# Layer 3's transfers of changed-over keys and queries issued by SP instead of GpSimd

## The chip, the core and the metric

The kernel is one program on one core of a Trainium2 chip. The core has five engines that run their own instruction streams in order and wait for each other through semaphores: TensorE (PE, with its weight loads shown apart as PEld), VectorE (DVE), ScalarE (ACT), GpSimd (POOL) and SyncE (SP), which here does nothing but issue transfers. Transfers (DMAs) are issued by SP or by GpSimd and carried out by 16 DMA engines. The metric is the time of the program on the device in microseconds (us); lower is better. All data are float32.

## What is computed

The input `x` has 4 batches of 1024 rows of 256 numbers. Four layers follow each other, each as `x = x + f(layernorm(x))`: attention (layer 1), a feed-forward net (layer 2), a second attention (layer 3), the same feed-forward net (layer 4). The change is in layer 3, whose core is:

```python
h = layernorm(x) * ln_scale + ln_bias              # 256 wide
c_q, c_kv = h @ w_down_q.T, h @ w_down_kv.T        # 128 wide
q, k, v = c_q @ w_up_q.T, c_kv @ w_up_k.T, c_kv @ w_up_v.T   # 16 heads of 64
e, o = q[..., 0::2], q[..., 1::2]                  # q, and k in the same way
q = interleave(e * cos - o * sin, e * sin + o * cos)
attn = softmax(q @ k.T / 8)
out = (attn @ v) @ w_out.T + residual
```

The rotation in the fifth line needs, beside each element of a query or key, its neighbour in the pair (even with odd). It is this exchange that is called changed over here.

## The kernel before

**Tiling.** Both attention layers are made by the same function, `attention` (L181). It takes two heads at a time (a pair of heads; 8 of them in each of the 4 batches, so 32 pairs in a layer), with keys and queries held transposed: 128 partitions (two heads of 64) by 1024 positions. A pair has 8 steps, each of 128 query rows, so a layer has 256 steps. Two steps make a half, called `h` in the code, and the unit in which transfers go.

**A step.** `scores` (L229) multiplies queries with keys into PSUM; `exponentials` (L244) finds the negated maximum on DVE (L249) and the exponential on ACT (L251); `invert` (L257) makes the reciprocal sums; `turn` (L265) transposes the probabilities in 32x32 blocks on DVE (L271) into the tile `T`. The blocks are then in the wrong partitions, so the 16 squares of a half are moved by DMA, each 32 partitions of 4352 bytes, 136 KB, from `T` to `pT` (`send`, L289, issued at L295). In layer 3 one square is copied by ACT instead (`keep`, L285), 10 are issued by SP and 5 by GpSimd (`POOL_DMA = 5`). In layer 1 it is 11 and 5. `weigh` (L297) multiplies `pT` with the values, two halves later; `take` (L310) scales the sums on GpSimd (L316); `project` (L318) multiplies with the output weights (L167) and adds to `x` on GpSimd (L328).

**Order.** Nothing is scheduled by the compiler: each engine runs its instructions in the order in which the Python code emits them, and waits are put in where data or buffers demand it. The loop in `steps_with` (L330) emits a step; other work (projections of the next pair, loads of weights) is put between by a table `pieces` from step number to functions. A piece at a whole number is emitted last in its step; a piece at a number that is `EARLY` = 0.5 smaller is emitted earlier in the step, ahead of `weigh`, `take`, `turn` and the sending. In the odd steps these lines matter:

```python
            for f in pieces.get(s - EARLY, ()):
                f()
            ...
            if part == 0 and 0 <= s < n:
                send(s // HB, nc.sync, sent[: len(sent) - POOL_DMA])
            for f in pieces.get(s, ()):
                f()
```

GpSimd's five squares of that half are emitted in the next, even step, after its `scores` and ahead of `project`.

**Buffers.** `T` and `pT` have two buffers each. So the first transposition of a half must wait until all 15 squares of the half before last have been read out of their `T`, and the first square of a half must wait until `weigh` and `take` are through with the `pT` of the half before last. The tile `turned` has one buffer.

**Keys and queries of layer 3.** `pair_b` (L630) prepares the next pair during the steps of the present one. `load` (L633) brings three weight tiles by SP; `load_out` (L208) brings the output weights, also three transfers, also by SP. For keys (i = 1) and then queries (i = 0), each in two blocks of 512 positions, it does `qk` (L638: a product and a copy by ACT, L647), `change` (L649: two DMAs of 64 partitions of 2048 bytes, 128 KB each, that exchange even and odd partitions into `turned`) and `rotate` (L654: three operations on GpSimd, L657 to L659, with tables of cosine and sine). `qk` is at k - EARLY, `change` at k + 1, `rotate` at k + 2, with k = -2, 0, 2 and 4: one block in every two steps. The steps of `change` are odd. Both weight loads are also pieces of odd steps, at EARLY, each in one of the four odd steps of a pair.

Of the kernel before, what the change touches and what calls it, by code (L numbers as in the profile page):

```python
# [35 lines left out]
EARLY = 0.5  # L36
# [3 lines left out]
def hybrid_block_kernel(  # L40
# [5 lines left out]
    nc = tc.nc  # L46
# [12 lines left out]
    def group(*shape):  # L59
        last[0] ^= 1  # L60
        return ps_mm.tile([P, *shape], F32, tag=f"m{last[0]}", name="mm")
# [84 lines left out]
    def standardize(dst, src, shift, rstd):  # L146
        nc.scalar.activation(dst, src, AF.Identity, scale=rstd, bias=shift)  # L147

    def transposed(dst, src, c, affine=None):

        tr = group(TQ, P)
        for t in range(TQ):
            nc.tensor.transpose(tr[:, t, :], src[:, t, ts(c, P)], ident)  # L153
        trf = tr.rearrange("p t q -> p (t q)")
        if affine is None:
            nc.scalar.copy(dst[:, c, :], trf)  # L156
        else:
            nc.scalar.activation(
                dst[:, c, :], trf, AF.Identity,
                scale=affine[0][:, c : c + 1], bias=affine[1][:, c : c + 1],  # L160
            )

    def paired(out, parts, first=True, last=True):

        for i, (lhsT, rhs) in enumerate(parts):
            for j in range(2):
                nc.tensor.matmul(  # L167
                    out[ts(j, DH)], lhsT[:, ts(j, DH)], rhs[j],
                    start=(first and i == 0), stop=(last and i == len(parts) - 1),
                )  # L170

    def by_head(out, parts):

        for i, (lhsT, rhs) in enumerate(parts):
            for j in range(2):
                nc.tensor.matmul(  # L176
                    out[ts(j, DH)], lhsT, rhs[:, ts(j, DH)],
                    start=(i == 0), stop=(i == len(parts) - 1),
                )
# [404 lines left out]
    def layer_b(rows):  # L584

        scale_b = 1.0 / 8.0
        cs = {}

        def batch_b(b):
            work = []  # L590
            for qb in range(NQB):
                k = {}

                def first(t, b=b, k=k, qb=qb):
                    if t == 0:
                        if b:
                            k["x1"] = xnp.tile([P, TQ, D], F32, tag="xn", name="x1")
                        else:
                            k["x1"] = ptp.tile([P, SENT], F32, tag="pT", name="x1")[
                                :, : TQ * D  # L600
                            ].rearrange("p (t d) -> p t d", t=TQ)
                    xt = xs[b][:, qb * TQ + t, :]
                    standardize(k["x1"][:, t, :], xt, *rows.factors(NQB * b + qb, t)[:2])
                    nc.gpsimd.tensor_add(xt, xt, k["x1"][:, t, :])

                def second(t, b=b, k=k, qb=qb):
                    x1 = k["x1"][:, t, :]
                    nc.scalar.mul(x1, x1, rows.factors(NQB * b + qb, t)[2])

                def turned(c, b=b, k=k, qb=qb):  # L610
                    if c == 0:
                        p, tag = (highp, f"high{qb}") if b % 2 == 0 else (lowp, "low")
                        cs[b, qb] = p.tile([P, NC, QB], F32, tag=tag, name="hc")
                    transposed(cs[b, qb], k["x1"], c, affine=(lns_sb, lnb_sb))

                def down(m, b=b, qb=qb):

                    h = cs[b, qb][:, :, ts(m, QB // 2)]
                    pc = group(2, QB // 2)
                    for i in range(2):  # L620
                        paired(pc[:, i], [(wd_sb[:, i, c, :], [h[:, c]] * 2) for c in range(NC)])
                    nc.scalar.copy(h, pc)

                work += [(10 * qb - 8 + t, lambda t=t, f=first: f(t)) for t in range(TQ)]
                work += [(10 * qb - 6 + t, lambda t=t, f=second: f(t)) for t in range(TQ)]
                work += [(10 * qb - 2 + 2 * c - EARLY, lambda c=c, f=turned: f(c)) for c in range(NC)]
                work += [(((2, 8), (16, 18))[qb][m], lambda m=m, f=down: f(m)) for m in range(2)]
            return work

        def pair_b(b, pr):  # L630
            made, turned = {}, {}

            def load():  # L633
                w = made["w"] = wp.tile([P, 3, NC, P], F32, tag="w", name="w")[:, :, 0, :]
                for i, up in enumerate((wuq, wuk, wuv)):
                    nc.sync.dma_start(w[:, i], up[:, ts(pr, P)])  # L636

            def qk(i, qb):  # L638

                pq = group(QB)  # L640
                paired(pq, [(made["w"][:, i, :], [cs[b, qb][:, i]] * 2)])
                name = ("qT", "kT")[i]
                if qb == 0:
                    made[name] = qkp.tile([P, S], F32, tag=name, name=name)
                straight = made[name][:, ts(qb, QB)]
                made[i, qb] = straight
                nc.scalar.mul(straight, pq, (scale_b, 1.0)[i])  # L647

            def change(i, qb):  # L649
                turned[i, qb] = rp.tile([P, QB], F32, tag="turned", name="turned")  # L650
                for r in range(2):
                    nc.gpsimd.dma_start(turned[i, qb][r::2], made[i, qb][1 - r :: 2])

            def rotate(i, qb):  # L654

                straight, other = made[i, qb], turned.pop((i, qb))
                nc.gpsimd.tensor_mul(straight, straight, cos_sb[:, ts(qb, QB)])  # L657
                nc.gpsimd.tensor_mul(other, other, sin_sb[:, ts(qb, QB)])
                nc.gpsimd.tensor_add(straight, straight, other)  # L659

            def values(qb):
                if qb == 0:
                    made["v"] = vp.tile([P, NK2, DH], F32, tag="v", name="v")
                pv = group(NK2 // NQB, DH)
                for t in range(NK2 // NQB):
                    lhsT = cs[b, qb][:, 1, ts(t, DH)]
                    by_head(pv[:, t, :], [(lhsT, made["w"][:, 2, :])])
                nc.scalar.copy(made["v"][:, ts(qb, NK2 // NQB), :], pv)

            work = []  # L670
            for i in (1, 0):
                for qb in range(NQB):
                    k = 2 - 4 * i + 2 * qb
                    work += [(k - EARLY, lambda i=i, qb=qb: qk(i, qb))]
                    work += [(k + 1, lambda i=i, qb=qb: change(i, qb))]
                    work += [(k + 2, lambda i=i, qb=qb: rotate(i, qb))]
            work += [(4 + 2 * qb - EARLY, lambda qb=qb: values(qb)) for qb in range(NQB)]
            return {name: lambda name=name: made[name] for name in ("qT", "kT", "v")}, load, work

        return attention(batch_b, pair_b, wo_b, nc.sync, lead=5, kept=1)  # L680


# [73 lines left out]
```

## Time and profile before

| What | us |
|---|---|
| median of 3 runs | 3290.56 (3285.77 to 3292.66) |
| profiled execution, whole | 3286.08 |
| profiled execution, span | 3284.2 |
| steady part of layer 3 in the span | 1700 to 3040 |

In 1700 to 3040 the busy times are: TensorE 1296.20, VectorE 1217.16, GpSimd 1170.68, ScalarE 1017.49 us of 1340, with a DMA share of 0.88. TensorE's granted clock is 0.99 there.

The whole span has this by engine, and this by transfers (columns of the second: name of the tile written and read, engine that issues, number, size of one, median time from the start of the issue to landing):

```profile
PE 3204.3 (98%) x52736; PEld 2022.2 (62%) x52736; DVE 2531.7 (77%) x2386; ACT 2107.9 (64%) x4304; POOL 1958.5 (60%) x2738
```

```profile
pT<-T SPq DMA_DIRECT2D x2688, 136.0 KB, 4.7
pT<-T POOLq DMA_DIRECT2D x1280, 136.0 KB, 4.8
turned<-kT POOLq DMA_DIRECT2D x128, 128.0 KB, 3.5
turned<-qT POOLq DMA_DIRECT2D x128, 128.0 KB, 3.3
...
wo<-in_wo_b SPq DMA_DIRECT2D x32, 128.0 KB, 3.7
```

The busy share of TensorE is no measure of how close it is to its limit, since the ends of pipelined matmuls are modelled. Issues by SP are not counted as busy anywhere: the page shows SP only in the chain of waits (as SPq) and in the list of transfers, and the timeline shows when it issued what.

### The profile page before, as it was taken

To read this page: it belongs to the slowest core of one execution; us is meant where nothing else is said; L and a number is where in the kernel's file an instruction comes from. 1 tells how busy PE (TensorE), PEld (TensorE's weight loads), DVE (VectorE), ACT (ScalarE), POOL (GpSimd) and SP (SyncE) were. 2 spreads that over 40 slices of the span, in tenths; PEclk is the share of its full clock that TensorE was granted. 3 is DMA by queue.
4 is the path that set the end of the run, shared out by engine and by line. 5 is a ranking of instruction groups with operands and counts; after the bars stand their busy time and mean duration, and the time that the engine had idled before them with its cause. 6 is when DMAs were issued, how large, how long until landed. Compare 5 with 4: busy or idle time off the path is not lost.

```text
span 3284.2 us, 126564 instructions
## 1 busy us (share of the span) xinstructions
PE 3204.3 (98%) x52736; PEld 2022.2 (62%) x52736; DVE 2531.7 (77%) x2386; ACT 2107.9 (64%) x4304; POOL 1958.5 (60%) x2738
## 2 busy tenths in 40 slices
PE   8999999999999999999999999999999999998999
PEld 4666666666666666666555556666666666655666
DVE  7988888888888888941049889998999899998100
ACT  5666666666666666643447877787777777777332
POOL 4545454445544544430158889998889898986110
PEclk9999999999999999999999999999999999999999
DMA  8888888888888888840039889988888899987100
GB/s 227 226 218 219 223 225 221 221 220 229 222 216 217 224 221 227 216 112 1 4 87 238 222 222 243 244 240 231 237 237 239 232 246 244 241 240 212 39 20 20
DMA packets 244698, 642.13 MB, mean 196 GB/s; under 512 B 74305, under 2 KB 102977, under 8 KB 244129
## 3 DMA queue, kind: packets, MB, share of 16 engines
q1 hardware_dynamic: 161104, 397.60, 47.4%
q0 software_dynamic: 83024, 236.44, 25.6%
q8 instruction: 419, 6.86, 1.0%
q14 instruction: 151, 1.23, 0.1%
HBM read 43.39 MB, written 4.19 MB: 14 GB/s over the span
## 4 chain that ended last, share of the span: by engine, by line
PE 71%; SPq 12%; DMA 6%; DVE 4%; ACT 4%; issue 3%; POOL 1%; DVEq 0%; ACTq 0%; POOLq 0%
PE sc L238 20%; PE mm L304 19%; PE mm L167 15%; SPq L295 11%; PE mm L421 7%; PE ph L410 7%; DMA pT<-T 5%; PE mm L176 4%; DVE T L271 2%; DVE nmax L249 1%; ACT p L251 1%; POOL oT L316 1%; PE mm L153 1%; ACT gT L414 0%; SPq L636 0%
## 5 line engine op out<-in xcount | busy, mean ns | idle before, releaser
L249 DVE TENSOR_REDUCE nmax<-sc 128x1 f32<-128x1024 f32 x1024 | 1204.3, 1218 | 222.8 <-PE sc L238 219.7
L251 ACT ACTIVATE p<-sc,nmax 128x1024 f32<-128x1024 f32 x1024 | 1144.1, 1117 | 323.0 <-DVE nmax L249 323.0
L271 DVE STREAM_TRANSPOSE T<-p 128x2176 f32<-128x2176 f32 x512 | 1247.4, 2436 | 50.9 <-DMA pT<-T 24.6
L238 PE MATMUL sc<-kT,qT 64*64 64x512 f32 x8192 | 1087.2, 598 | 15.6 <-ACT p L251 10.5
L304 PEld LDWEIGHTS mm<-pT,v 64*64 64x64 f32 x32768 | 951.3, 133 | 141.7 <-issue 100.6
L304 PE MATMUL mm<-pT,v 64*64 64x128 f32 x32768 | 986.7, 269 | 10.3 <-issue 9.5
L295 POOL DMA_DIRECT2D pT<-T x1280 | 629.6, 499 | 120.8 <-PE sc L238 55.4
L316 POOL TENSOR_TENSOR oT<-oT,pT 128x256 f32<-128x256 f32 x256 | 186.2, 727 | 719.7 <-ACT oT L314 647.7
L238 PEld LDWEIGHTS sc<-kT,qT 64*64 64x64 f32 x8192 | 333.8, 133 | 413.8 <-issue 276.1
L328 POOL TENSOR_TENSOR x<-x,got 128x512 f32<-128x512 f32 x256 | 330.9, 1293 | 26.9 <-ACT got L326 22.9
L326 ACT COPY got<-mm 128x512 f32<-128x512 f32 x256 | 149.8, 585 | 282.0 <-PE mm L167 282.0
L428 DVE TENSOR_TENSOR x<-x,mm 128x512 f32<-128x512 f32 x32 | 22.0, 687 | 367.1 <-PE mm L421 367.1
L167 PE MATMUL mm<-wo,oT 128*64 128x256 f32 x2048 | 278.4, 393 | 19.9 <-POOL oT L316 18.7
L167 PEld LDWEIGHTS mm<-wo,oT 128*64 128x64 f32 x2048 | 124.6, 136 | 267.3 <-POOL oT L316 221.5
L260 ACT COPY p<-total 128x128 f32<-128x128 f32 x512 | 151.8, 297 | 203.7 <-DVE total L259 197.1
L414 ACT ACTIVATE gT<-ph,b_sb 128x512 f32<-128x512 f32 x128 | 87.4, 685 | 299.6 <-PE ph L410 299.5
L167 PE MATMUL mm<-hT,w 128*64 128x512 f32 x1024 | 243.3, 596 | 1.1 <-ACT hT L156 1.0
L421 PE MATMUL mm<-w_sb,gT 128*128 128x256 f32 x1024 | 226.0, 381 | 6.5 <-ACT hT L156 6.5
L410 PE MATMUL ph<-hT,w_sb 128*128 128x512 f32 x512 | 229.3, 601 | 0.2 <-ACT hT L156 0.2
L421 PEld LDWEIGHTS mm<-w_sb,gT 128*128 128x128 f32 x1024 | 193.1, 190 | 39.4 <-ACT hT L156 9.4
L396 POOL TENSOR_TENSOR x<-x,b_sb 128x256 f32<-128x256 f32 x64 | 44.5, 726 | 275.5 <-ACT xn L147 275.5
L251 ACT ACTIVATION_READ_ACCUMULATOR p<-sc,nmax 128x1 f32 x1024 | 205.0, 200 | 0.0
(90 smaller groups left out, 2471.4 us busy)
## 6 DMA issues: line engine op xcount, KB each, us to landing
pT<-T SPq DMA_DIRECT2D x2688, 136.0 KB, 4.7
pT<-T POOLq DMA_DIRECT2D x1280, 136.0 KB, 4.8
turned<-kT POOLq DMA_DIRECT2D x128, 128.0 KB, 3.5
turned<-qT POOLq DMA_DIRECT2D x128, 128.0 KB, 3.3
w<-in_wqkv_a POOLq DMA_DIRECT2D x96, 128.0 KB, 5.9
wo<-in_wo_a POOLq DMA_DIRECT2D x32, 128.0 KB, 5.1
wo<-in_wo_a POOLq DMA_DIRECT2D x64, 64.0 KB, 5.3
wo<-in_wo_b SPq DMA_DIRECT2D x32, 128.0 KB, 3.7
```

The source lines that it names most:

```text
L167: nc.tensor.matmul(out[ts(j, DH)], lhsT[:, ts(j, DH)], rhs[j], start=(first and i == 0), stop=(last and i == len(parts) - 1),)
L238: nc.tensor.matmul(sc[s, j][ts(half, DH), ts(m, 512)], qT()[rows, ts(2 * qs + half, DH)], kT()[rows, ts(m, 512)], start=True, stop=True,)
L249: nc.vector.tensor_reduce(nmax, sc[s, j], AX.X, ALU.max, negate=True)
L251: nc.scalar.activation(probs[s][:, :NK2, ts(j, 2), :], sc.pop((s, j)).rearrange("p (k c i) -> p k c i", c=2, i=SQ), AF.Exp, bias=nmax, acc ...
L260: nc.scalar.copy(probs[s][:, NK2].rearrange("p (j c) i -> p j (c i)", j=2), t.unsqueeze(2).to_broadcast([P, 2, DH]),)
L271: nc.vector.transpose(T[h][:, :, q, :, :].rearrange("p c k i -> p k c i"), probs.pop(s))
L295: engine.dma_start(pT[h][ts(c, SQ), a], T[h][ts(a, SQ), c])
L304: nc.tensor.matmul(av[h][q][ts(j ^ q, DH)], v[ts(j, DH), k, :], pT[h][ts(j, DH), :, q, k, :], start=(k == 0), stop=(k == NK2 - 1),)
L316: nc.gpsimd.tensor_mul(parts, parts, pT.pop(h)[:, :, :, NK2, :])
L328: nc.gpsimd.tensor_add(xd, xd, got)
L410: nc.tensor.matmul(ph, w1_sb[:, c, ts(f, P)], hT[n][:, c, :], start=(c == 0), stop=(c == NC - 1),)
L421: nc.tensor.matmul(po[n][:, t % 2, :], gT[n][:, f, ts(t, P)], w2_sb[:, f, :], start=(f == 0), stop=(f == NF - 1),)
```

## The change

`change` issues its two DMAs from SP (`nc.sync`) instead of GpSimd, and its place in the table goes from k + 1 to k + 1 - EARLY. It so stands in SP's stream ahead of the 10 squares of the same odd step and behind the 10 squares of the half before. Where an odd step also has a load, the three loads of output weights come ahead of `change`, and the three loads of the projection's weights behind it. Shapes, bytes, buffers and arithmetic stay as they are.

```diff
             def change(i, qb):
                 turned[i, qb] = rp.tile([P, QB], F32, tag="turned", name="turned")
                 for r in range(2):
-                    nc.gpsimd.dma_start(turned[i, qb][r::2], made[i, qb][1 - r :: 2])
+                    nc.sync.dma_start(turned[i, qb][r::2], made[i, qb][1 - r :: 2])
...
                     work += [(k - EARLY, lambda i=i, qb=qb: qk(i, qb))]
-                    work += [(k + 1, lambda i=i, qb=qb: change(i, qb))]
+                    work += [(k + 1 - EARLY, lambda i=i, qb=qb: change(i, qb))]
                     work += [(k + 2, lambda i=i, qb=qb: rotate(i, qb))]
```

## The prediction

> **What bounds the kernel now.** The change touches layer 3 alone, so I read the page for the whole span first and then each view for 1700 to 3040 us, the steady part of layer 3. The 254 transpositions (L271) in it start between 1700.7 and 3034.6: 5.27 us a step, 42.2 us a pair of heads, some 31.8 pairs. VectorE needs per step two maxima of 1.22, a transposition of 2.44 and a reciprocal of 0.12, 5.0 us: 95% of the step. So VectorE is nearly the bound, and what the kernel loses is 0.27 us a step in which it waits for others. Who these are, the chain of waits in that window tells first (shares by engine and line; SPq is SP issuing):
>
> ```profile
> by line: SPq L295 27.0%; PE sc L238 14.7%; PE mm L304 12.8%; DMA pT<-T 11.1%; PE mm L167 9.0%; issue 6.2%; DVE T L271 3.6%; DVE nmax L249 2.7%; ACT p L251 2.4%; PE mm L176 1.4%; POOL oT L316 1.2%; SPq L636 0.8%; SPq L214 0.7%; DMA w<-in_wuq
> ```
>
> SP's issuing of squares leads, with their flight behind it; GpSimd has 1.2%. The groups of L295 in the window (ns: least, median, most) show that a square costs SP anything from 0.5 to 2.3 us, and GpSimd always the same:
>
> ```profile
> L295 SPq DMA_DIRECT2D pT<-T x1270: 507/597/2333, 1699.1 to 3039.9; - x182
> L295 POOL DMA_DIRECT2D pT<-T x635: 489/492/553, 1709.0 to 3039.6; - x159
> ```
>
> The waits of SP in the window (total us, times, longest) show how little of SP is free, and the timeline of SP alone what it does in two pairs (start, us, what):
>
> ```profile
> SPq L295 <- DVE total L259: 57.0, 46, 3.5
> SPq L295 <- POOL oT L316: 14.8, 17, 3.5
> SPq L295 <- DVE T L271: 6.7, 3, 3.1
> SPq L295 <- DMA pT<-T: 4.6, 9, 0.9
> SPq L214 <- DMA pT<-T: 4.1, 6, 0.9
> ```
>
> ```profile
> 2347.70 20.04 SPq L295 DMA_DIRECT2D pT<-T  x20
> 2367.78 0.59 SPq L212 DMA_DIRECT2D wo<-in_wo_b  x1
> 2368.42 1.18 SPq L214 DMA_DIRECT2D wo<-in_wo_b  x2
> 2369.90 17.63 SPq L295 DMA_DIRECT2D pT<-T  x20
> ```
>
> With 1.5 us of smaller rows all its waits are 88.7 us of 1340: 2.8 us a pair. SP is issuing for the other 93%. Most of the free time lies in the two odd steps of a pair that have no load; where one has (half of them), the row after it shows the squares starting at once, late. And late squares cost: the next transposition but one half needs its tile read out. The waits of VectorE and TensorE in the window:
>
> ```profile
> DVE T L271 <- DMA pT<-T: 15.2, 21, 2.0
> ...
> DVE T L271 <- DMA wo<-in_wo_b: 3.3, 4, 1.3
> ```
>
> ```profile
> PE mm L167 <- POOL oT L316: 17.9, 25, 3.3
> ```
>
> With three smaller rows for landings of weights (which use the same semaphores) the transpositions lose 21.0 us. Where they lose nothing the margin is small: from the last landing of a half to the start of the transposition that needs its tile the median over 122 halves of the trace is some 0.7 us.
>
> **The change part by part.**
>
> *GpSimd loses 8 issues a pair.* The median is 0.570 us, so 256 are 146 us, in layer 3 1.14 us of every two steps (10.55 us), of which GpSimd is busy 87% (1170.68 of 1340). It isn't on the path except where it is late for L316: the 17.9 us above, in 25 places. Being 1.14 us earlier should take about half of that away, the other places being the batch edges, where it is up to 3.3 us late: **-9 us**. Its five squares start earlier by the same 1.14 us; they have 4 us to spare before their tile is needed, so that gains nothing.
>
> *SP gets 8 issues a pair.* No row has SP issuing a transfer of 64 partitions of 2048 bytes. From below the nearest is L214 (64 partitions of 1024 bytes, median 0.594, least 0.502), from above a square under pressure, 0.88 (below). I take 0.60, as they stand where the queue is emptiest, with 0.04 to the next, and one instruction of 0.06 for a wait a step: 5.4 us a pair. By the ends it is 4.6 to 7.5.
>
> *The squares behind them.* The bytes are the same, but 262 KB a half leave GpSimd's queue, where they ran together with SP's squares. The windows of the transfers show what that may do (the last columns are the share of the DMA engines and GB/s):
>
> ```profile
> 2335.00:2337.00 2.00, 2.00 (x21) 0.73 (x15) 1.90 (x3) 1.79 (x6) 1.30 (x4) 1.00 0.49 122
> ...
> 2339.00:2341.00 2.00, 2.00 (x19) 0.88 (x21) 1.57 (x1) 1.94 (x5) 1.98 (x3) 1.00 1.02 275
> ```
>
> Just ahead of a half's squares the DMA engines are half idle, and 2 us into them they are full, and this is what makes a square cost SP more than 0.6. 262 KB at 275 GB/s are 1.0 us: the most that ten squares can gain if all pressure is one pool of bytes. The least is nothing. Layer 1 is the row between: there GpSimd issues five squares a half and no changes. In 200 to 1400 SP waits 177.4 us and issues 1209 squares: (1200 - 177.4)/1209 = 0.846 us each with all gaps. In layer 3, with its 183 loads at a mean of 0.68 and 0.04 of gap, it is (1340 - 88.7 - 132)/1270 = 0.881. So a half without the changes in GpSimd's queue is 10 x 0.035 = 0.35 us shorter; I take that, since it is measured on the same squares: -1.4 us a pair (ends: 0 and -4.0).
>
> *What SP waits for.* `change` waits for ACT's copy (L647), made in the step before and finished some 5 us earlier, and for L659 to be through with `turned`. L659 ended 0.7 us or more before the first square of its step, median about 2; relieved of the issues it ends up to 1.1 us sooner, while SP wants to issue 1.3 us ahead of the squares. So mostly no wait; but what there is holds up ten squares queued behind it, which nothing did before. `rotate` waits for the landing: 18.5 us in 23 places now (L657), off the path; the transfer now leaves 1 to 2 us sooner. Nothing.
>
> *The first four blocks*, made before layer 3's steps, cost SP about what they cost GpSimd: 0.
>
> *Sum.* SP needs 5.4 - 1.4 = 4.0 us a pair more and has 2.8: the pair gets 1.2 us longer, x 31.8 = **+38 us**, less 9 = **+29 us**. What bounds then is SP: 43.4 us a pair. On the profiled execution: 3286.1 + 29 = 3315; the median of the runs shown lies 4.5 higher: 3290.6 + 29 = **3320**.
>
> **A rule against the rows.** The Trainium skill, DMA: Bandwidth & Descriptors, section "Issuing engines are not separate DMA queues", says that transfers from any engine run on the same 16 DMA engines, and that the choice of the issuer saves only sequencer time, which is usually small beside the transfer. By it the move is worth GpSimd's 9 us at best, and SP's 5.4 us a pair would hide: 3282. The rows say that here the sequencer's time is not small: a square's issue is 0.88 of a flight of 4.8, and SP has 2.8 us a pair to give. The same page ("Specifications") has the first byte about 0.4 us sooner from SP. The rows have 3.7 us to landing for 128 KB from SP (L212) and 3.3 to 3.5 for the changes from GpSimd: no gain. I follow the rows in both.
>
> **Rivals.**
>
> *A. SP saturates* (forecast, 0.46). 3298 to 3345: 0.6 to 1.7 us a pair.
>
> *B. The pressure goes with the burst; faster* (0.27). The changes move into the half-idle 2 us, and ten squares get about 1.0 us shorter. SP then needs 5.4 - 4.0 = 1.4 us a pair, which fits in its 2.8. Squares land earlier, of VectorE's 21.0 us half go (the rest turns into waits for scores), with half of the 17.9: -19, **3271**; all of both would be 3252. For it speaks the 0.49 above, against it that layer 1, without changes, still pays 0.846. It decides from a gain of (5.4 - 2.8)/4 = 0.65 us a half.
>
> *C. Both fit* (0.10): a gain near 0.65: 3285 to 3296, **3291**.
>
> *D. SP's free time can't be used and the tile's wait holds SP* (0.17). In the two loaded steps of a pair SP has nothing free, so both halves go 1.3 us later, the other two 0.3: 3.2 us a pair; 0.7 of the margin is spent once. 3.2 x 31.8 x 0.8 = +81: **3372**; the few places in which GpSimd is late would then hold the squares up as well. Against it: a longer pair eases the pressure on the DMA engines.
>
> **Numbers.** The likeliest is A, 3320; its own range is 3298 to 3345. Two kernels can be told apart from about 0.2%, 6.6 us. Faster is B, 0.27; same is C, 0.10; slower is A and D, 0.63. The range for 8 in 10 takes in most of B and of D: 3262 to 3378.
>
> **What would show it.** In the profile after, A has: SP's waits for VectorE and GpSimd nearly gone (under 1 us a pair), squares at about 0.85 each, the transposition's waits for landings over 40 us, the pair at 43 us or more, L316's hold on TensorE near half. B has SP's waits kept and squares under 0.80. D has rows in which SP's issue of `turned` waits for L659. I am wrong if squares get shorter by 0.65 us a half or more, or if SP's issue of a change is far from 0.60.

## The result, and the profile after

| | before | after |
|---|---|---|
| median, us (4 runs each) | 3288.61 | 3326.53 |
| ratio, 95% interval | | 1.0118 (1.0105 to 1.0130) |
| span of the profiled execution | 3284.2 | 3321.3 |
| 254 transpositions of layer 3, first start to last | 1333.9 | 1369.0 |
| a pair of heads | 42.2 | 43.3 |

The kernel is 38 us slower. Of the 37.1 us between the two spans, 35.1 lie in layer 3, between its first and its last transposition. Below, layer 3 after is 1700 to 3077 us. The page after, by engine and by transfers, shows GpSimd 132 us less busy than before, and the changes with SP's name:

```profile
PE 3209.7 (97%) x52736; PEld 2024.8 (61%) x52736; DVE 2535.5 (76%) x2386; ACT 2111.5 (64%) x4304; POOL 1826.7 (55%) x2482
```

```profile
pT<-T SPq DMA_DIRECT2D x2688, 136.0 KB, 4.3
pT<-T POOLq DMA_DIRECT2D x1280, 136.0 KB, 4.3
turned<-kT SPq DMA_DIRECT2D x128, 128.0 KB, 3.5
turned<-qT SPq DMA_DIRECT2D x128, 128.0 KB, 3.3
```

A change takes 3.5 us (keys) and 3.3 us (queries) to land from either engine. What differs is when it is issued, and what waits for it. GpSimd's waits for the changes in layer 3 before (total us, times, longest):

```profile
POOL qT L657 <- DMA turned<-qT: 9.7, 12, 1.4
POOL kT L657 <- DMA turned<-kT: 8.8, 11, 1.4
```

The waits in layer 3 after, first TensorE's, then GpSimd's, then those of the transpositions for landings, then SP's own:

```profile
PE mm L167 <- POOL oT L316: 52.2, 46, 3.7
```

```profile
POOL kT L657 <- DMA turned<-kT: 83.2, 32, 4.5
...
POOL qT L657 <- DMA turned<-qT: 31.6, 20, 4.1
```

```profile
DVE T L271 <- DMA pT<-T: 11.5, 13, 3.0
DVE T L271 <- DMA turned<-kT: 11.1, 12, 2.1
DVE T L271 <- DMA wo<-in_wo_b: 4.3, 6, 1.9
...
DVE T L271 <- DMA turned<-qT: 2.3, 4, 1.3
```

```profile
SPq L295 <- DVE total L259: 9.5, 9, 2.3
SPq L652 <- POOL oT L316: 7.7, 19, 0.9
SPq L652 <- POOL kT L659: 6.1, 12, 1.3
```

TensorE's wait for L316 was 17.9 us and is 52.2. The wait of `rotate` for the changes was 18.5 and is 114.8. The transpositions' wait for landings was 21.0 and is 29.2 (a wait is put down to a square, a load or a change from SP, whichever came last, so all such rows count as one wait). SP's own waits fell from 88.7 to 37.0 us, or from 2.8 to 1.2 a pair; the largest row left is 9.5.

Where a change is late is shown by the timeline, of SP alone and then of GpSimd alone (start, us, what, and in brackets the idle time before it):

```profile
2340.45 0.58 SPq L212 DMA_DIRECT2D wo<-in_wo_b  x1
2341.07 1.15 SPq L214 DMA_DIRECT2D wo<-in_wo_b  x2
2342.34 1.16 SPq L652 DMA_DIRECT2D turned<-kT  x2
2343.80 7.39 SPq L295 DMA_DIRECT2D pT<-T  x10
2351.55 1.15 SPq L652 DMA_DIRECT2D turned<-kT  x2
```

```profile
2340.46 0.72 POOL L316 TENSOR_TENSOR oT<-oT,pT 128x256 f32<-128x256 f32 x1
2341.47 2.48 POOL L295 DMA_DIRECT2D pT<-T  x5 [0.30 <-POOL oT L316]
2343.97 1.29 POOL L328 TENSOR_TENSOR x<-x,got 128x512 f32<-128x512 f32 x1
2347.65 1.28 POOL L657 TENSOR_TENSOR kT<-kT,cos_sb 128x512 f32<-128x512 f32 x1 [2.39 <-DMA turned<-kT]
2348.88 1.29 POOL L658 TENSOR_TENSOR turned<-turned,sin_sb 128x512 f32<-128x512 f32 x1
2350.25 1.27 POOL L659 TENSOR_TENSOR kT<-kT,turned 128x512 f32<-128x512 f32 x1
2351.49 0.71 POOL L316 TENSOR_TENSOR oT<-oT,pT 128x256 f32<-128x256 f32 x1
```

The three loads of output weights stand ahead of the change, so it leaves SP at 2342.34, 1.2 us after the L316 of the step. GpSimd is through with L328 at 2345.3 and stands idle for 2.4 us. The three operations of `rotate` then end where the next L316 starts, and on that L316 TensorE's L167 waits. In the traces the four blocks of a pair compare so (medians over some 30 pairs, us from the end of the L316 of the step, before and after):

| block | issued | landed | total idle time ahead of `rotate` |
|---|---|---|---|
| keys, first (behind the loads) | -0.1, 1.2 | 4.5, 6.8 | 7.9, 73.1 |
| keys, second | -0.1, -0.7 | 4.2, 2.2 | under 1, 9.0 |
| queries, first | -0.1, -0.9 | 3.9, 2.4 | 1.4, 9.3 |
| queries, second | -0.1, 0.3 | 4.4, 4.6 | 6.9, 25.6 |

GpSimd is ready for `rotate` at 4.8 before and 4.4 after. So the first block of keys lands 2.4 us too late, and the second block of queries just too late. Only the first weighs: in the trace after, 35.0 of the 52.2 us that TensorE waits for L316 come right behind the `rotate` of that block (4.2 of 17.9 before). The change does leave sooner where SP is free, and later where it isn't.

### The profile page after: what moved, and what is told of

It reads as the page before. It is cut to its first block, busy times and chain, and to the rows that moved or that the text cites. A ratio compares the mean times of both kernels' runs of the same rounds, so it can differ in the third digit from the quotient of the medians.

```text
span 3321.3 us, 126690 instructions
## 1 busy us (share of the span) xinstructions
PE 3209.7 (97%) x52736; PEld 2024.8 (61%) x52736; DVE 2535.5 (76%) x2386; ACT 2111.5 (64%) x4304; POOL 1826.7 (55%) x2482
## 2 busy tenths in 40 slices
DMA packets 252890, 642.14 MB, mean 193 GB/s; under 512 B 74304, under 2 KB 102976, under 8 KB 252320
## 4 chain that ended last, share of the span: by engine, by line
PE 70%; SPq 14%; DMA 6%; POOL 3%; issue 3%; ACT 2%; DVE 2%; POOLq 0%; ACTq 0%; DVEq 0%
PE sc L238 20%; PE mm L304 19%; PE mm L167 14%; SPq L295 11%; PE mm L421 7%; PE ph L410 7%; PE mm L176 4%; DMA pT<-T 4%; SPq L652 1%; DMA turned<-kT 1%; POOL oT L316 1%; POOL pT L295 1%; DVE T L271 1%; DVE nmax L249 1%; ACT p L251 1%
## 5 line engine op out<-in xcount | busy, mean ns | idle before, releaser
L271 DVE STREAM_TRANSPOSE T<-p 128x2176 f32<-128x2176 f32 x512 | 1247.3, 2436 | 66.4 <-DMA pT<-T 19.2
L238 PE MATMUL sc<-kT,qT 64*64 64x512 f32 x8192 | 1089.8, 599 | 12.7 <-ACT p L251 11.4
L238 PEld LDWEIGHTS sc<-kT,qT 64*64 64x64 f32 x8192 | 336.0, 133 | 413.9 <-issue 280.7
L316 POOL TENSOR_TENSOR oT<-oT,pT 128x256 f32<-128x256 f32 x256 | 185.9, 726 | 723.0 <-ACT oT L314 670.8
L328 POOL TENSOR_TENSOR x<-x,got 128x512 f32<-128x512 f32 x256 | 330.9, 1293 | 26.9 <-ACT got L326 23.0
L167 PE MATMUL mm<-wo,oT 128*64 128x256 f32 x2048 | 278.5, 393 | 53.8 <-POOL oT L316 53.1
L167 PEld LDWEIGHTS mm<-wo,oT 128*64 128x64 f32 x2048 | 124.4, 136 | 301.6 <-POOL oT L316 255.9
L167 PE MATMUL mm<-hT,w 128*64 128x512 f32 x1024 | 243.4, 596 | 1.0 <-ACT hT L156 1.0
```

The costliest lines, as they stand in the source:

```text
L167: nc.tensor.matmul(out[ts(j, DH)], lhsT[:, ts(j, DH)], rhs[j], start=(first and i == 0), stop=(last and i == len(parts) - 1),)
L238: nc.tensor.matmul(sc[s, j][ts(half, DH), ts(m, 512)], qT()[rows, ts(2 * qs + half, DH)], kT()[rows, ts(m, 512)], start=True, stop=True,)
L271: nc.vector.transpose(T[h][:, :, q, :, :].rearrange("p c k i -> p k c i"), probs.pop(s))
L316: nc.gpsimd.tensor_mul(parts, parts, pT.pop(h)[:, :, :, NK2, :])
L328: nc.gpsimd.tensor_add(xd, xd, got)
```

## The experiments

All ratios are against the kernel before, on the same chip, with 95% intervals. "L316" is TensorE's wait for it, "landings" the transpositions' wait, in us, of 1700 to 3060 (the windows named above for before and after; 1800 to 3700 for the last row). The waits are those of one execution of each kernel, the profiled one, which in a_rot_late is 13 us below the median of its runs and in b_pool3 9 us above. An edit that adds or takes a line shifts the numbers: L314, L317 or L318 is L316 there, L269 or L272 is L271.

| label | edit | ratio | L316 | landings |
|---|---|---|---|---|
| before | | 1 | 17.9 | 21.0 |
| after | the change | 1.0118 (1.0105-1.0130) | 52.2 | 29.2 |
| a_swap | after, change ahead of the loads | 1.0107 (1.0091-1.0124) | 25.1 | 58.7 |
| a_wo_late | after, loads behind the squares | 1.0124 (1.0108-1.0140) | 49.4 | 36.9 |
| a_pool6 | after, GpSimd sends 6 squares | 1.0087 (1.0071-1.0102) | 54.2 | 14.6 |
| b_pool4 | before, GpSimd sends 4 | 0.9998 (0.9989-1.0008) | 14.6 | 27.7 |
| a_swap_pool6 | both edits | 1.0032 (1.0020-1.0044) | 21.3 | 24.7 |
| b_pool3 | before, GpSimd sends 3 | 1.0086 (1.0072-1.0100) | 17.7 | 62.2 |
| a_rot_late | after, rotate behind L316 | 1.0182 (1.0165-1.0200) | 21.4 | 121.0 |
| b_rot_late | before, rotate behind L316 | 1.0081 (1.0067-1.0095) | 18.1 | 81.5 |
| a_swap_pool7 | as a_swap, GpSimd sends 7 | 1.0024 (1.0017-1.0032) | 21.2 | 17.5 |
| a_loads_pool | after, loads by GpSimd | 0.9993 (0.9982-1.0004) | 20.4 | 23.4 |
| b_early | the place alone | 1.0024 (1.0016-1.0031) | 28.9 | 12.7 |
| a_behind | the queue alone | 1.2326 (1.2301-1.2350) | 566.3 | 0.4 |

**Theories.** Two can explain the loss. S: SP is saturated; its number of issues sets the time of a pair, since late squares hold up the transposition that needs their tile. R: the change lands late behind the loads, so `rotate` is late, so L316 behind it is late, and TensorE waits for L316.

**a_swap.**

```diff
-            pieces.setdefault(NT * g - 1 - EARLY, []).append(lambda g=g: load_out(g))
...
             for k, f in work:
...
+            for o in [g - 1] * (g > 0) + [g] * (g == len(pairs) - 1):
+                pieces.setdefault(NT * o - 1 - EARLY, []).append(lambda o=o: load_out(o))
```

> The changed kernel (1.0118 of before, +38 us), with one order turned round: in the one odd step of a pair that has both, the change of keys is issued ahead of the three loads of output weights and no longer behind them. What SP issues, and when its squares start, stays the same. Theory S (SP is saturated, the number of its issues sets the pair): no gain, 1.010 to 1.013. Theory R (the change lands late there, so rotate on GpSimd is late, so L316 is late and TensorE waits): TensorE's wait for L316 goes from 52 us back to about 20, GpSimd's wait of L657 for keys from 83 us to under 20, and the ratio to about 1.003 (+10 us).

TensorE's wait went nearly as R said, from 52.2 to 25.1, and the time stayed as S said. R had also put GpSimd's wait for keys under 20 us; it stayed at 59.4, since the lateness only moved to other blocks. TensorE's, GpSimd's and the transpositions' waits in this run:

```profile
PE mm L167 <- POOL oT L317: 25.1, 44, 1.9
```

```profile
POOL kT L658 <- DMA turned<-kT: 59.4, 31, 4.2
POOL qT L658 <- DMA turned<-qT: 54.0, 28, 3.9
```

```profile
DVE T L272 <- DMA pT<-T: 35.1, 18, 3.8
...
DVE T L272 <- DMA turned<-kT: 12.6, 10, 2.3
DVE T L272 <- DMA turned<-qT: 11.0, 9, 2.8
```

The last three are 58.7 us, for 29.2 with the loads ahead. The first block of keys now lands at 3.7, but the two blocks after a step with loads land at 6.0 and 6.2: late for `rotate`, but less so than 6.8, and they held TensorE by only 7 and 8 us. So neither theory is right alone: a second wait seems to stand close beside the first and to take its place, which a_swap_pool6 tests.

**a_wo_late.**

```diff
-            pieces.setdefault(NT * g - 1 - EARLY, []).append(lambda g=g: load_out(g))
+            pieces.setdefault(NT * g - 1 - (EARLY if kept == 0 else 0), []).append(lambda g=g: load_out(g))
```

> The changed kernel with the three loads of output weights moved behind the ten squares of their step, so that both the change and the squares of that step go 1.8 us sooner and the next step's change bears the loads. S: SP issues as much as in the changed kernel, so no gain: 1.010 to 1.013. R: the late landing moves to the next block of keys (k = 0), behind the squares and the loads, so about half is won: 1.006.

No gain. The late landing moved whole to the next block of keys (issued at 1.5, landed at 6.8, 66 us of idle time ahead of `rotate`; 28.6 of L316's 49.4 us come right behind it), where R had expected to win half.

**a_pool6, b_pool4, b_pool3** set the number of squares that GpSimd sends in layer 3:

```diff
+        n_pool = 6 if kept else POOL_DMA
...
-                    send(s // HB - 1, nc.gpsimd, sent[len(sent) - POOL_DMA :])
+                    send(s // HB - 1, nc.gpsimd, sent[len(sent) - n_pool :])
...
-                    send(s // HB, nc.sync, sent[: len(sent) - POOL_DMA])
+                    send(s // HB, nc.sync, sent[: len(sent) - n_pool])
```

> The changed kernel with six squares a half from GpSimd and nine from SP in layer 3: SP is relieved of 4 x 0.83 = 3.3 us a pair, of the 4 us or so that the change added; GpSimd gets 4 x 0.5 = 2.0 us of the 4.6 that it saved. S: nearly all comes back, 0.998 to 1.003. R: SP's changes go up to 0.8 us sooner, but the three loads still stand ahead of one of four, and rotate starts 0.5 us later on GpSimd; a third comes back: 1.008.

> The kernel before (changes on GpSimd) with four squares a half from GpSimd and eleven from SP in layer 3: SP gets 4 x 0.85 = 3.4 us a pair, about what the change gave it, but nothing that rotate waits for is in its queue. S: SP is as full as in the changed kernel, so 1.006 to 1.012. R: rotate isn't late and GpSimd is relieved by 2.0 us a pair, so 0.999 to 1.003.

> The kernel before with three squares a half from GpSimd and twelve from SP in layer 3. With eleven SP's waits fell from 89 to 39 us and the time stayed (0.9998). With twelve SP needs 8 squares a pair more, some 5 to 6 us, over the 2.8 that it has free, more than in the changed kernel. Saturation alone, with nothing for rotate in SP's queue: 1.008 to 1.020, all of it in the transpositions' waits for landings and none in L316. If SP's issue gives way (a square costs less the longer the queue has had to drain), under 1.004.

a_pool6 is the counterpart of a_swap: landings fall to 14.6, below before, and L316 stays at 54.2, for the change still stands behind the loads. It wins a quarter of the loss, near the third that R expected and far from S. b_pool4 gives SP an eleventh square and costs nothing, as R expected: SP's waits shrink to 39.0 us, and its squares get cheaper to issue (below). A twelfth is too much, with nothing for `rotate` in SP's queue. The transpositions' waits of b_pool3:

```profile
DVE T L271 <- DMA pT<-T: 48.7, 25, 4.5
...
DVE T L271 <- DMA wo<-in_wo_b: 5.5, 3, 4.0
```

So S is real by itself, and sets in between eleven squares, which cost nothing, and twelve, which cost 0.86% with L316 at 17.7.

**a_swap_pool6** has both edits.

> The changed kernel with both edits: the change of keys ahead of the output weights' loads, and six squares a half from GpSimd. Turning the order round alone gave 1.0107 (the wait of TensorE for L316 went, that of the transpositions for landings came), moving the square alone 1.0087 (the other way round). If two paths stand side by side, each of which holds the kernel at about +35 us (a late change through rotate and L316; late squares through the transposition's tile), both edits together bring nearly all back: 0.997 to 1.003, with TensorE's wait for L316 under 20 us and the transpositions' waits under 35. If the loss is one thing that neither edit touches (a rotate that hangs on SP at all), 1.006 or more.

Turning the order round won 0.1%, which is within the noise, moving the square 0.3%, both 0.9%. Two waits side by side explain that: either alone holds the kernel near the same time. 0.3% are left; the ratio and L316 lie just above what was expected for two paths (1.003, and 20 us), the landings below.

**a_swap_pool7.**

> The changed kernel with the change of keys ahead of the output weights' loads and seven squares a half from GpSimd, eight from SP: with six it was 1.0032. SP then issues as many transfers a half as before the change (8 + 2), GpSimd 7 as before (7 + 0). If what is left of the loss is SP's load, 0.998 to 1.001; if it is the tie between rotate and SP's queue, which this leaves, 1.002 to 1.005.

It stays at 1.0024. Here SP waits 111 us in all, and most of that is for the one buffer of `turned` (L661 is L659):

```profile
SPq L654 <- POOL qT L661: 44.2, 32, 4.7
SPq L654 <- POOL kT L661: 30.7, 27, 4.0
```

That is the tie between `rotate` and SP's queue, as the second half of the expectation had it: 75 us of waits with squares queued behind. Whether they make up the 0.24% stays open: no run has the changes on SP with a second buffer of `turned` and nothing else altered.

**a_loads_pool** leaves the changes on SP and takes the six loads off it.

```diff
-                pieces.setdefault(NT * g - NT - lead - EARLY, []).append(load)
+                pieces.setdefault(NT * g - NT - lead - (EARLY if kept == 0 else 0), []).append(load)
...
-                    nc.sync.dma_start(w[:, i], up[:, ts(pr, P)])
+                    nc.gpsimd.dma_start(w[:, i], up[:, ts(pr, P)])
...
-        return attention(batch_b, pair_b, wo_b, nc.sync, lead=5, kept=1)
+        return attention(batch_b, pair_b, wo_b, nc.gpsimd, lead=5, kept=1)
```

(`load_out` is placed as in a_wo_late.)

> The changed kernel with all six weight loads of a pair in layer 3 issued by GpSimd, at the end of their step: SP gives away 6 x 0.66 = 4.0 us a pair of the 5.4 that the changes brought, no change stands behind a load, and GpSimd gets 6 x 0.55 = 3.3 us of the 4.6 that it saved. Two paths that come from SP's load: 0.998 to 1.004. If a change in SP's queue is bad in itself, 1.006 or more.

All comes back. TensorE and the transpositions wait about as before the change:

```profile
PE mm L167 <- POOL oT L316: 20.4, 31, 2.0
```

```profile
DVE T L271 <- DMA pT<-T: 12.5, 9, 3.1
DVE T L271 <- DMA turned<-qT: 8.5, 11, 1.3
...
DVE T L271 <- DMA turned<-kT: 2.4, 5, 1.1
```

So a change in SP's queue is not bad in itself, once the loads leave that queue. The run takes away both causes at once, SP's load and the loads ahead of a change, and so doesn't tell them apart. It isn't faster than before within the interval; no version that ran beats the kernel before.

**a_rot_late and b_rot_late** put L316 ahead of `rotate` on GpSimd. Both leave out the second bias of the feed-forward layers and add another tile in its place, of the same size.

```diff
-                turned[i, qb] = rp.tile([P, QB], F32, tag="turned", name="turned")
+                turned[i, qb] = rp.tile([P, QB], F32, tag=f"turned{qb}", name="turned")
...
-                    work += [(k + 2, lambda i=i, qb=qb: rotate(i, qb))]
+                    work += [(k + 3, lambda i=i, qb=qb: rotate(i, qb))]
...
-                nc.gpsimd.tensor_add(xt, xt, b2_sb)
+                nc.gpsimd.tensor_add(xt, xt, cos_sb[:, :D])
```

> The changed kernel with rotate a step later (k + 3), so that GpSimd does L316 ahead of it and a late change can't hold L316 up; turned has two buffers for that. To make room the second bias of the feed-forward layers is replaced by the first 256 columns of the table of cosines, so those sums are changed and their time is not. Two paths: TensorE's wait for L316 goes under 15 us, but SP's squares are as late as ever, so 1.006 to 1.011 with the transpositions' waits at 50 us or more. If the path through rotate is all: 0.998 to 1.003.

> The kernel before with the same later rotate and the same exchanged bias: changes on GpSimd. It is the control of the run of the changed kernel with later rotate. TensorE's wait for L316, 17.9 us, should fall under 10; GpSimd's five squares go 2 to 4 us later and have 4 to spare. 0.996 to 1.002.

Both missed upwards, because the edit itself costs 0.8%: GpSimd's five squares of a half now follow 3.8 us of `rotate`, and of their 4.2 us of margin 0.8 are left in the control (medians of the traces; landings 81.5). A wait that no other run has comes with it, in both: the first scores of a pair now wait for the last `rotate` of its queries (L657 is L659, L236 is L238), 24.5 us with the change and 24.1 in the control:

```profile
PE sc L236 <- POOL qT L657: 24.1, 28, 1.6
```

L316, expected under 15 and 10 us, stayed at 21.4 and 18.1, but in waits of at most 0.3 and 0.7. Against its control the change costs 1.0182/1.0081 = 1.010 here too. L316 and the new wait differ by 3.3 and 0.4 us between the two, the landings by 39.5 (121.0 and 81.5): here late landings carry the loss nearly alone.

**b_early and a_behind** are the two halves of the change.

> The place alone: changes by GpSimd as before, at k + 1 - EARLY. On GpSimd they then stand ahead of L316 of the same step and no longer behind it. The copies that they wait for are done, so they are issued in GpSimd's free time of 0.6 us ahead of L316 and hold L316 up by some 0.5 us in every two steps; TensorE's wait for L316 grows from 18 us to 40 or more. 1.001 to 1.010.

> The queue alone: changes by SP at k + 1, behind the ten squares of their step. SP's issues are the same in number; the change leaves SP about 9 us later and lands some 12 us after L316, where rotate was ready at 4.4. Rotate, in order on GpSimd ahead of the next L316, holds that up by several us in every two steps: a pair of 50 us or more, 1.06 to 1.16. If only SP's number of issues counted, 1.012.

The place alone costs 0.24%, with L316 late by 11 us more, less than expected. The queue alone costs 23%, above the expected range (6 to 16%). GpSimd's and TensorE's waits there:

```profile
POOL kT L657 <- DMA turned<-kT: 457.6, 56, 9.6
POOL qT L657 <- DMA turned<-qT: 455.0, 57, 9.7
```

```profile
PE mm L167 <- POOL oT L316: 566.3, 112, 7.8
```

The change lands some 12 us after L316, as expected; GpSimd then idles 8 us in each half, and no block escapes. The pair is 67.5 us. This is R without S (landings 0.4), and it says why the place had to go with the queue. How much of the 23% is R stays open, since TensorE's clock was lower too (below).

## Why the prediction was right, and where it wasn't

It forecast 3320 and +29 us through a full SP; measured are 3326.5 and +38. The direction and the size hold; the mechanism is half of what was measured, and that the size fits is partly luck, as the terms show. Rival D's mark is faint: SP's issues of changes wait for GpSimd, that is for L659 (some of it put down to GpSimd's next operations), for 16.1 us in all.

*What bounds.* That SP's time is scarce is confirmed by b_pool3 (two more squares a half on SP cost 0.86%) and by a_swap (with TensorE's wait for L316 back at 25.1 us, the landings hold the kernel). The reading of 93% was too high: of the 42.2 us of a pair before, issues took 36.5 and waits 2.6; the rest is gaps between the issues.

*SP gets 8 issues.* Taken at 0.60; the median is 0.594, the mean 0.63. With the gaps they add 5.4 us a pair. Right.

*The squares behind them.* The term was a gain of 1.4 us a pair. The mean issue of a square went from 815 to 755 ns, so 40 are 2.4 us cheaper: between the row of layer 1 and the bound by bytes. Rival B needed 0.65 us a half and got 0.6; it came close to its point of decision. That full DMA engines make the issue dear isn't shown: when the squares of the trace before are sorted into fifths by the DMA share of the 2 us ahead of each, the emptiest fifth (0.49) took a mean of 687 ns and the fullest (1.04) 784, but the middle one (0.92) 937.

*SP's 2.8 us of free time.* The sum used all of it and expected under 1 to be left; 1.2 are. So the pair's +1.2 us came out almost exact by two errors that cancel: 5.4 - 2.4 - 0.2 (six loads, cheaper by 36 ns each) - 1.6 = 1.2. That is luck. With these measured terms SP needed 2.8 us more a pair and had 2.8: by the prediction's own sum both would have fitted, as in rival C. That the pair got longer all the same, the runs put down to the two waits together: the late change at L316, and squares that come late behind more issues.

*The step that failed* is the wait of `rotate` for the landing, taken as "off the path; the transfer now leaves 1 to 2 us sooner. Nothing." Two blocks of four do leave sooner, by 0.6 and 0.8 us. The order of the pieces, which the text ahead of the prediction itself gave, puts three loads ahead of the first block of keys; that change leaves 1.3 us later than before, and `rotate`, in front of L316 on the same engine, puts it on TensorE's path: the wait of `rotate` went from 18.5 to 114.8 us. With it fell the -9 us: L316's hold didn't halve, it tripled. And the forecast that over 40 us of landings would show was not met (29.2), because the wait at L316 came first and hid it: a_swap brought it out (58.7).

*The range of A.* Its ends in time, 3298 to 3345, and in a pair, 0.6 to 1.7 us, don't belong together throughout: 1.7 us are 54, and less the 9 us they give 3336.

*The rule.* By the Trainium skill, DMA: Bandwidth & Descriptors, "Issuing engines are not separate DMA queues", all issuers share the same 16 DMA engines and only the issuer's time is at stake; the move would have been worth 9 us at best. The runs bear out that the flight is no different: a change lands 3.5 and 3.3 us after its issue from either engine, and in the blocks made ahead of layer 3's steps, with no squares in flight, 1.9 to 2.0 us after it from GpSimd and 1.9 to 2.1 from SP. But the issuer's time, and the moment at which it comes round to the change, cost 1.2% of the kernel.

## What to carry to other kernels

A queue that only issues transfers can be among the fullest engines of a kernel without a busy time anywhere on the page: add up its waits, and set what is free against what is to be added. Before a transfer is moved into another queue, list what stands ahead of it in every step, not in the typical one: here one block of four made most of the loss at L316. And when a wait goes and the time stays, look for the wait that took its place; two side by side have to be taken away together.

## What the runs showed of the hardware

SP's time for issuing the same 136 KB square isn't fixed. In four runs it falls as SP sends more squares of a half and GpSimd fewer: a mean of 847 ns with 8 from SP and 7 from GpSimd (a_swap_pool7), 815 with 10 and 5 (before), 779 with 11 and 4 (b_pool4), 746 with 12 and 3 (b_pool3). That is the relief by which SP took an eleventh square for nothing. The numbers of squares alone don't set it, though: with the same 10 and 5 it is 733 in b_rot_late, where GpSimd's first square goes out 4.8 us after SP's first (a median, 0.9 before), and 746 in a_swap, where it goes 2 us ahead. In the trace before, squares issued with at most 5 other transfers in flight took a mean of 628 ns, those with 10 or more 973. This fits a cost that rises where the two queues' squares overlap in time; what makes it rise isn't shown. GpSimd's median for a square stays between 489 and 496 ns.

The same change goes in other packets: the page counts 244698 packets before and 252890 after, since a change from GpSimd goes in packets of 4096 bytes and from SP in packets of 2048. The landing is as fast either way.

In a_behind the mean granted clock of TensorE over the whole span was 0.908, where it was 0.997 before, and in layer 3 (1700 to 3800) it was 0.82, where it was 0.99. The run in which TensorE waits most also got the lowest clock, so part of its 23% may be that; it wasn't taken apart.
